# A graph and expert layer on one core: first norms, turns and weights by halves of the features, and six key tiles on the first two token tiles

## The chip, the cores and the metric

The kernel runs on one core of a Trainium2 chip. The metric is device microseconds of one execution; shown are three runs. A core has TensorE (PE; its weight loads are listed apart as PEld), VectorE (DVE), ScalarE (ACT), GpSimd (POOL) and SyncE (SP), which here only issues transfers. Each engine takes its instructions in the order in which the built program holds them, and waits on semaphores of the others.

## What is computed

A layer on 625 tokens of 1024 features, with 20000 edges: a layer norm, then two graph convolutions and a linear attention beside them, added to the input, then a second layer norm and a mixture of 8 experts with a shared one. Cut to what matters here:

```python
xn = _layernorm(x)
x = x + gnn(xn, src, dst) + mix(xn)          # two mean-over-neighbours layers; linear attention
x = x + moe(_layernorm(x))
# in mix:   k = softmax(xn @ Wk over the tokens), q = softmax(xn @ Wq over a head's features)
# in gnn:   h = relu(xn @ W_self0 + mean(xn) @ W_neigh0 + b0), then the same with W_self1, W_neigh1
# in moe:   the best 2 of 8 experts of softmax(xf @ router_w), silu(xf @ w1[e]) @ w2[e],
#           plus sigmoid(xf @ shared_gate_w) * (silu(xf @ gate) * (xf @ up)) @ shared_down
```

## The kernel before, in words

Nearly all products are made in float32r with both factors split into a high part and a rest: `split` (L98 to L99) casts the high part on ACT and subtracts it on DVE, which leaves the rest. A product is then three matmuls: high by high, high by rest, rest by high. Names ending in h and hi are high parts, in l and lo rests. `Stream` (L102 to L130) loads weights in tiles of 128x1024 through SP, three ahead, into the three buffers `wraw`, and `next()` splits the next tile into `whi` and `wlo`, three buffers of each.

Tokens come in five tiles of 128 (the last of 113). The head of the kernel, L433 to L462, is written out by hand. For each token tile `first_stats` and `first_scale` make the norm's factors on DVE (with a root on ACT), `first_norm` (L336) applies them on DVE or ACT in place in `xts`, and `first_turn` (L344, through `to_t`, L283) transposes the tile on PE in two groups of four 128x128 blocks and splits each group into `xnh` and `xnl` (features on the partitions). Before that PE runs 34 matmuls on zeros (L251) as a warm-up.

The keys' product, 8 tiles of 128 output features by Wk and 8 more by W_self0, is cut into 64 half steps (`keys_step`, L391): step s takes output tile o, token part i and half h of the features, 12 matmuls. For the first four output tiles the parts are tokens 0 to 255 and 256 to 625 (256 and 370 columns), and all four go over the first part (steps 0 to 7) before any goes over the second (8 to 15), so the first part needs two token tiles alone. Later tiles use 384 and 242 columns. The fourth tile's weights have a place of their own, `fourth`. `keys_steps` (L418) also starts, some steps behind, the exp of a finished key tile (`keys_exp`) and its transpose back (`keys_back`). `kbuf` holds four key tiles. Beside the steps DVE makes 160 pairs of one-hot tiles from the edges (`one_hots`, L493: four after each of steps 8 to 15, then three a step), which PE counts in groups of 16 (`count_group`).

The order of issue on each engine is chosen when the program is built, by a planner that takes instructions by their place in the program (higher inside `tc.high_priority()`) as soon as its own estimates say that their inputs are there. Two means bind it: `tc.keep_in_program_order` (called `keep`) puts an instruction behind the one written just before it on its engine, and `tc.issue_after(ins)` puts a block's instructions on the engine of `ins` behind `ins`. In the head all of DVE's work and all of ACT's but the copies into `kbuf` are kept; the keys' matmuls and the transposes of the edges (`turn_edges`, L354) are not.

After the second norm, `logits` (L946) makes the router's 2x16 small matmuls (20 output rows, 314 and 312 columns), after all of the first shared tile's products (L965 to L974). Experts are taken by rank in the order 0, 1, 2, 6, 3, 4, 5, 7. `expert_wide` (L1193) first makes `he` (matmuls into `pse`), splits it, then makes the second product in eight quarter steps (into `psy`, L1231 on). The next expert's rows are turned meanwhile by a `Turn` (L1016), one `step()` before each weight tile: a 32x32 transpose on DVE (L1046) into `raw`, whose split goes to ACT and POOL. An expert of 128 rows is turned on PE.

Of the kernel before, what the change touches and what calls it, by code (L numbers as in the profile page):

```python
# [19 lines left out]
N = 625  # L20
# [25 lines left out]
RANKS = (0, 1, 2, 6, 3, 4, 5, 7)  # L46
WARM = 34
# [26 lines left out]
def gps_layer(ctx: ExitStack, tc: tile.TileContext, x, src, dst,  # L74
# [27 lines left out]
    class Stream:  # L102
# [24 lines left out]
        def next(self, eng=None, into=None, **order):  # L127
            i = self.used
            self.used += 1
            self.load(max(i + self.ahead, i + 1))  # L130
            ap = self.todo[i]
            r = self.raw.pop(i)
            if into is not None:
                hi, lo = into
            else:
                hi = wts.tile([128, D], F32R, name="whi", tag="whi")
                lo = wts.tile([128, D], F32R, name="wlo", tag="wlo")
            split(r, hi, lo, eng, **order)
            b = ap.shape[2]
            return (hi.rearrange("p (a b) -> p a b", b=b), lo.rearrange("p (a b) -> p a b", b=b))  # L140
# [142 lines left out]
    def to_t(nat, t, hi, lo, order=None, both={}):  # L283
        for g in range(2):
            ps = bank("pst").rearrange("p (a b) -> p a b", b=128)
            for k in range(4):
                kt = 4 * g + k
                tr = nc.tensor.transpose(ps[:, k, rows(t)], nat[:, kt], ident[rows(t), rows(t)])
# [47 lines left out]
    def first_norm(t, eng):  # L336
        p = rows(t)
        y, z = lnt[p, 0, t:t + 1], lnt[p, 1, t:t + 1]
        if eng is nc.vector:
            keep(nc.vector.tensor_scalar(xts[p, t, :], xts[p, t, :], y, z, op0=ALU.mult, op1=ALU.add))  # L340
        else:
            keep(nc.scalar.activation(xts[p, t, :], xts[p, t, :], AF.Identity, bias=z, scale=y))

    def first_turn(t):  # L344
        return to_t(xts[rows(t), t, :].rearrange("p (k c) -> p k c", c=128), t, xnh, xnl, keep, dict(order=keep))
# [18 lines left out]
    kbuf = big.tile([128, 4, NP], F32, name="kbuf", tag="big")  # L364

    fourth = big.tile([128, 2, D], F32R, name="fourth", tag="big")
# [6 lines left out]
    def keys_back(o):  # L373
        ke = kbuf[:, o % 4, :N]
# [7 lines left out]
    def keys_exp(o):  # L382
        ke = kbuf[:, o % 4, :N]
# [7 lines left out]
    def keys_step(s):  # L391
        o, i, h = s // 4, s // 2 % 2, s % 2
        if s < 16:
            o, i = s // 2 % 4, s // 8
        if (o, i, h) == (1, 1, 0):
            wks[4] = st.next()
        if i == 0 and h == 0 and 3 < o < 2 * KT - 1:
# [4 lines left out]
        c0, n = ((0, 2 * T), (2 * T, NP - 2 * T))[i] if o < 4 else SPARTS[i]  # L402
        c, ps = slice(c0, c0 + n), kps[0]
        for kt in range(4 * h, 4 * h + 4):
            nc.tensor.matmul(ps[:, :n], wh[:, kt, :], xnh[:, kt, c], start=kt == 0, stop=False)  # L405
            nc.tensor.matmul(ps[:, :n], wh[:, kt, :], xnl[:, kt, c], start=False, stop=False)  # L406
            nc.tensor.matmul(ps[:, :n], wl[:, kt, :], xnh[:, kt, c], start=False, stop=kt == KT - 1)  # L407
        if h == 1:
            n = min(n, N - c0)
            if o < KT:  # L410
                nc.scalar.copy(kbuf[:, o % 4, c0:c0 + n], ps[:, :n])
# [17 lines left out]
    def keys_weights(o):  # L429
        wks[o] = st.next(into=(fourth[:, 0, :], fourth[:, 1, :]) if o == 3 else None, order=keep)  # L430


    with tc.high_priority():  # L433
# [27 lines left out]
        last = first_turn(4)  # L461
        keys_steps(1)  # L462
# [66 lines left out]
    while ks[0] < 8 * KT:  # L529
# [5 lines left out]
        one_hots(3)  # L535
# [6 lines left out]
    ath = atp.tile([128, NT, XP], F32R, name="ath")  # L542
# [403 lines left out]
    def logits():  # L946
        for c0, n in PARTS:
# [22 lines left out]
    to_t(by_k(xfn[rows(4), 4, :]), 4, xfh, xfl)  # L970
    ga.append(bank("psga"))
# [3 lines left out]
    logits()  # L975
# [40 lines left out]
    class Turn:  # L1016


        def __init__(self, row, n):
            self.n, self.xb, self.xs, self.left = n, expert_load(row, n), None, None  # L1020
            self.todo = [(t0, g) for t0 in range(0, n // 32, 4) for g in range(2)]

        def step(self):
# [17 lines left out]
            else:  # L1041
# [4 lines left out]
                tc.keep_in_program_order(nc.vector.transpose(  # L1046
                    raw.rearrange("p k (t r) -> p t k r", r=32), rows[:, :, k]))
# [145 lines left out]
    def expert_wide(row, n, xs, early, nxt, aside=None):  # L1193
# [5 lines left out]
        for q in range(KT // 2):  # L1199
# [24 lines left out]
            if beside:  # L1224
                nc.scalar.copy(h2[:, :, :n], s)
                for a0, b0, m in ((0, main, 128), (128, more, rest)):
                    nc.vector.tensor_sub(h2[:, :, b0:b0 + m], s[:, :, a0:a0 + m], h2[:, :, a0:a0 + m].bitcast(F32))
# [192 lines left out]
```

## Time and profile before

| | us |
|---|---|
| median of three runs | 1005.16 (1004.86 to 1005.45) |
| the profiled execution's own time | 1006.07 |
| its span, first to last instruction | 1004.5 |
| PE, PEld, DVE, ACT, POOL busy | 994.2, 860.1, 601.4, 394.4, 144.5 |

The page gives each engine's busy time as a share of the span, the granted clock (0.999 of full) and the groups of instructions by cost. A timeline line reads: start, duration, engine, line, operation, output<-inputs, shape out<-in, count of merged instructions, and in brackets the engine's idle time before and what ended it. A matmul's listed duration is longer than the distance to the next one, because they are pipelined; distances are taken from start to start.

### The profile page before, as it was taken

Reading aid. Unit: us, or ns where it says so; the run is one execution under the profiler, and the core shown is the slowest. Engines: PE = TensorE matmul, PEld = TensorE weight load, DVE = VectorE, ACT = ScalarE, POOL = GpSimd, SP = SyncE. Lnnn points to the kernel's source line nnn. Section 1 sums busy time; section 2 is a strip of 40 time slices with the busy share of each in tenths; the row PEclk is TensorE's granted clock in tenths of the full one; section 3 lists DMA queues with packets and bytes.
Section 4 is the critical chain, followed back from the end, with each engine's and each line's share of the span. In section 5 each row is a group of like instructions: output and inputs, shape, how many; then the busy total and the mean of one; then the engine's idle time right before and its main releaser. Section 6 shows DMA issues by size and latency. Waiting matters only on the chain. (4 is left out here: it accounts for less than half of the span.)

```text
span 1004.5 us, 14780 instructions
## 1 busy us (share of the span) xinstructions
PE 994.2 (99%) x5547; PEld 860.1 (86%) x5547; DVE 601.4 (60%) x1215; ACT 394.4 (39%) x577; POOL 144.5 (14%) x206
## 2 busy tenths in 40 slices
PE   9999999999999999999999999999999999999998
PEld 6999998888887779888878999997978787887886
DVE  7998745682333346423338355367678788877682
ACT  5533242231123212222116242265557576766610
POOL 1000011120100432200001002223032203110040
PEclk9999999999999999999999999999999999999999
DMA  8222227762321343322220125766977997887961
GB/s 238 60 65 64 85 100 257 251 235 86 95 84 64 105 157 124 124 83 84 66 82 2 46 81 173 241 205 207 266 244 217 292 357 237 280 297 253 339 249 64
DMA packets 111596, 164.69 MB, mean 164 GB/s; under 512 B 5948, under 2 KB 63686, under 8 KB 111512
## 3 DMA queue, kind: packets, MB, share of 16 engines
q1 hardware_dynamic: 97864, 118.38, 36.7%
q0 software_dynamic: 13456, 45.08, 13.6%
q8 instruction: 46, 0.75, 0.3%
q14 instruction: 38, 0.31, 0.1%
q10 hardware_dynamic: 192, 0.16, 0.0%
HBM read 133.19 MB, written 30.42 MB: 163 GB/s over the span
## 5 line engine op out<-in xcount | busy, mean ns | idle before, releaser
L99 DVE TENSOR_TENSOR wlo<-wraw,whi 128x1024 fp32r<-128x1024 f32 x148 | 186.0, 1257 | 247.0 <-ACT whi L99 237.8
L99 ACT CAST whi<-wraw 128x1024 fp32r<-128x1024 f32 x148 | 155.5, 1051 | 288.1 <-PE psg L211 76.2
L1215 PE MATMUL pse<-xs,whi 128*128 128x448 f32 (+1 forms) x384 | 109.2, 357 | 0.0
L99 DVE TENSOR_TENSOR wlo<-wmore,whi 128x1024 fp32r<-128x1024 f32 x67 | 82.1, 1226 | 25.8 <-ACT whi L99 23.3
L1211 PE MATMUL pse<-xs,wlo 128*128 128x224 f32 (+1 forms) x384 | 89.5, 254 | 0.6 <-DVE wlo L99 0.6
L99 ACT CAST whi<-wmore 128x1024 fp32r<-128x1024 f32 x67 | 70.4, 1051 | 42.5 <-PE psz L211 18.3
L405 PE MATMUL psk<-xnh,whi 128*128 128x384 f32 (+3 forms) x240 | 74.5, 312 | 0.3 <-ACT xnh L99 0.3
L406 PE MATMUL psk<-xnl,whi 128*128 128x384 f32 (+3 forms) x240 | 73.5, 306 | 0.6 <-DVE xnl L99 0.6
L407 PE MATMUL psk<-xnh,wlo 128*128 128x384 f32 (+3 forms) x240 | 73.5, 306 | 0.0
L1211 PEld LDWEIGHTS pse<-xs,wlo 128*128 128x128 f32 x384 | 72.0, 190 | 1.6 <-DVE wlo L99 0.8
L1215 PEld LDWEIGHTS pse<-xs,whi 128*128 128x128 f32 x384 | 69.1, 189 | 2.4
L1269 PE MATMUL psy<-whi,he 128*128 128x512 f32 (+1 forms) x176 | 69.5, 395 | 0.7 <-PEq L1304 0.7
L1270 PE MATMUL psy<-wlo,he 128*128 128x512 f32 (+1 forms) x176 | 69.4, 394 | 0.7 <-DVE wlo L99 0.7
L1271 PE MATMUL psy<-whi,he 128*128 128x512 f32 (+1 forms) x176 | 69.0, 392 | 0.0
L488 DVE TENSOR_SCALAR hot<-iota,srow,unit 125x128 f16<-125x128 f16 x160 | 49.6, 310 | 0.0
L406 PEld LDWEIGHTS psk<-xnl,whi 128*128 128x128 f32 x240 | 45.5, 190 | 0.8 <-DVE xnl L99 0.8
L405 PEld LDWEIGHTS psk<-xnh,whi 128*128 128x128 f32 x240 | 45.4, 190 | 0.6 <-ACT xnh L99 0.6
L407 PEld LDWEIGHTS psk<-xnh,wlo 128*128 128x128 f32 x240 | 45.4, 189 | 0.0
L99 POOL TENSOR_TENSOR xs<-raw,xs 128x512 fp32r<-128x512 f32 (+2 forms) x24 | 28.3, 1182 | 110.0 <-ACT xs L99 109.6
L487 DVE TENSOR_SCALAR hot<-iota,edt 125x128 f16<-125x128 f16 x160 | 39.8, 250 | 4.1 <-PE pa L505 4.1
L1269 PEld LDWEIGHTS psy<-whi,he 128*128 128x128 f32 (+1 forms) x176 | 31.9, 181 | 10.8 <-issue 1.1
L1270 PEld LDWEIGHTS psy<-wlo,he 128*128 128x128 f32 (+1 forms) x176 | 31.8, 181 | 10.0 <-DVE wlo L99 1.7
(361 smaller groups left out, 2367.2 us busy)
## 6 DMA issues: line engine op xcount, KB each, us to landing
wraw<-in_L_ffn_w_dram SPq DMA_DIRECT2D x65, 512.0 KB, 5.1
wmore<-in_L_ffn_w_dram SPq DMA_DIRECT2D x63, 512.0 KB, 5.2
xsd<-zt POOLq DMA_DIRECT2D x9, 1024.0 KB
wraw<-in_L_gnn_W_self_dram SPq DMA_DIRECT2D x16, 512.0 KB, 3.6
wraw<-in_L_gnn_W_neigh_dram SPq DMA_DIRECT2D x16, 512.0 KB, 3.8
wraw<-_ffn_shared_gate_up_dram SPq DMA_DIRECT2D x16, 512.0 KB, 3.9
wraw<-in_L_mix_Wk_dram SPq DMA_DIRECT2D x8, 512.0 KB, 6.7
wraw<-in_L_mix_Wq_dram SPq DMA_DIRECT2D x8, 512.0 KB, 3.6
```

The lines of the kernel that those rows point to most:

```text
L99: return (order(nc.scalar.copy(hi, srcap)), order((eng or nc.vector).tensor_sub(lo, srcap, hi.bitcast(F32))))
L405: nc.tensor.matmul(ps[:, :n], wh[:, kt, :], xnh[:, kt, c], start=kt == 0, stop=False)
L406: nc.tensor.matmul(ps[:, :n], wh[:, kt, :], xnl[:, kt, c], start=False, stop=False)
L407: nc.tensor.matmul(ps[:, :n], wl[:, kt, :], xnh[:, kt, c], start=False, stop=kt == KT - 1)
L487: nc.vector.tensor_scalar(h[:ET, :WIN], iota[:ET, :WIN], edst[e], None, op0=ALU.is_equal)
L488: return nc.vector.tensor_scalar(h[:ET, WIN:], iota[:ET, :WIN], srow[e], unit[e].bitcast(F32), op0=ALU.is_equal, op1=ALU.mult)
L1211: nc.tensor.matmul(ps[a][:, :n], wl[:, k, c], xs[:, kt, 0, :], start=False, stop=False)
L1215: nc.tensor.matmul(ps[a][:, :2 * n], wh[:, k, c], xs[:, kt], start=kt == 0, stop=kt == KT - 1)
L1269: nc.tensor.matmul(acc, h(kt, 0), wh[:, k, :], start=kt == 0, stop=False)
L1270: nc.tensor.matmul(acc, h(kt, 0), wl[:, k, :], start=False, stop=False)
L1271: nc.tensor.matmul(acc, h(kt, 1), wh[:, k, :], start=False, stop=kt == KT - 1)
```

## The change

- `AHEAD = 6`: six instead of four output tiles of the keys go over the first two token tiles (steps 0 to 11) before the second part (steps 12 to 23). Tiles 3 to 5 have places of their own: two in `beside`, one in `sixth`, which lies where `ath` comes later. `kbuf` holds six tiles; exp and transpose back start eight steps later.
- The order of the three kinds of matmuls inside a step changes for these tiles: by kind, four features tiles at a time.
- In the head token tiles 0 and 1 are normed by halves of the features (three halves on DVE, one on ACT), turned by halves (both tiles' first half, then both tiles' second), and the first weight tile is split by halves, the second half between the two turns. The edges' cast, the other weights, statistics and norms are moved.
- One-hots: three after each of steps 12 to 23, then three and four in turns.
- The first 16 router matmuls come before the first shared tile's last products.
- A `Turn`'s transposes on DVE are queued behind the rest of the last weight tile taken and behind the rest of the last `he`.

```diff
+AHEAD = 6
...
-        def next(self, eng=None, into=None, **order):
+        def next(self, eng=None, into=None, apart=False, **order):
...
-            split(r, hi, lo, eng, **order)
             b = ap.shape[2]
-            return (hi.rearrange("p (a b) -> p a b", b=b), lo.rearrange("p (a b) -> p a b", b=b))
+            both = (hi.rearrange("p (a b) -> p a b", b=b), lo.rearrange("p (a b) -> p a b", b=b))
+            if apart:
+
+                return both, [lambda c=slice(i * 512, (i + 1) * 512): split(r[:, c], hi[:, c], lo[:, c], eng, **order)
+                              for i in range(2)]
+            self.low = split(r, hi, lo, eng, **order)[1].ins
+            return both
...
-    kbuf = big.tile([128, 4, NP], F32, name="kbuf", tag="big")
-
-    fourth = big.tile([128, 2, D], F32R, name="fourth", tag="big")
+    kbuf = big.tile([128, AHEAD, NP], F32, name="kbuf", tag="big")
+
+    beside = big.tile([128, 4, D], F32R, name="beside", tag="big")
+    sixth = atp.tile([128, 2, D], F32R, name="sixth", tag="ath")
+    places = [beside[:, i, :] for i in range(4)] + [sixth[:, i, :] for i in range(2)]
...
-        if s < 16:
-            o, i = s // 2 % 4, s // 8
+        if s < 4 * AHEAD:
+            o, i = s // 2 % AHEAD, s // (2 * AHEAD)
         if (o, i, h) == (1, 1, 0):
-            wks[4] = st.next()
-        if i == 0 and h == 0 and 3 < o < 2 * KT - 1:
+            wks[AHEAD] = st.next()
+        if i == 0 and h == 0 and AHEAD <= o < 2 * KT - 1:
             wks[o + 1] = st.next()
...
-        c0, n = ((0, 2 * T), (2 * T, NP - 2 * T))[i] if o < 4 else SPARTS[i]
+        c0, n = ((0, 2 * T), (2 * T, NP - 2 * T))[i] if o < AHEAD else SPARTS[i]
         c, ps = slice(c0, c0 + n), kps[0]
-        for kt in range(4 * h, 4 * h + 4):
-            nc.tensor.matmul(ps[:, :n], wh[:, kt, :], xnh[:, kt, c], start=kt == 0, stop=False)
-            nc.tensor.matmul(ps[:, :n], wh[:, kt, :], xnl[:, kt, c], start=False, stop=False)
-            nc.tensor.matmul(ps[:, :n], wl[:, kt, :], xnh[:, kt, c], start=False, stop=kt == KT - 1)
+        kts = range(4 * h, 4 * h + 4)
+        terms = ((wh, xnh), (wh, xnl), (wl, xnh))
+        if s < 2:
+
+            order = [(kt, *terms[j]) for j in (0, 2, 1) for kt in kts]
+        elif i == 0 and o < AHEAD:
+            order = [(kt, *terms[j]) for j in (0, 1, 2) for kt in kts]
+        elif i == 1 and o == 0:
+            order = [(kt, *terms[j]) for j in (0, 2) for kt in kts]
+            if h == 1:
+                order += [(kt, *terms[1]) for kt in range(KT)]
+        else:
+            order = [(kt, *term) for kt in kts for term in terms]
...
-            if 10 <= k < 4 * KT + 10 and k % 4 == 2:
-                keys_exp((k - 10) // 4)
-            if 14 <= k < 4 * KT + 14 and k % 4 == 2:
-                keys_back((k - 14) // 4)
+            if 18 <= k < 4 * KT + 18 and k % 4 == 2:
+                keys_exp((k - 18) // 4)
+            if 22 <= k < 4 * KT + 22 and k % 4 == 2:
+                keys_back((k - 22) // 4)
...
         first_scale(0, 2)
-        first_norm(0, nc.vector)
-        keys_weights(0)
-        first_norm(1, nc.scalar)
-        first_turn(0)
-        first_turn(1)
+
+        lower, upper = (slice(g * 512, (g + 1) * 512) for g in range(2))
+        wks[0], halves = st.next(order=keep, apart=True)
+        for t, c in ((0, lower), (1, lower), (1, upper)):
+            first_norm(t, nc.vector, c)
+        halves[0]()
+        first_norm(0, nc.scalar, upper)
+        for g in range(2):
+            if g:
+                halves[1]()
+            for t in range(2):
+                first_turn(t, (g,))
+        keys_weights(1)
         first_stats(2)
-        keys_weights(1)
-        keep(nc.scalar.copy(edges, ei))
         keys_weights(2)
         first_scale(2, 3)
+        keep(nc.scalar.copy(edges, ei))
         keys_steps(2)
+        first_norm(2, nc.scalar)
         turn_edges()
-        first_norm(2, nc.scalar)
+        keys_weights(3)
+        first_stats(3)
         keys_steps(2)
-        first_stats(3)
+        keys_weights(4)
         first_stats(4)
-        keys_weights(3)
         first_scale(3, 5)
         keys_steps(2)
         first_norm(3, nc.vector)
+        keys_weights(5)
+        first_norm(4, nc.scalar)
         first_turn(2)
-        keys_steps(1)
-        first_norm(4, nc.scalar)
+        keys_steps(4)
         first_turn(3)
         last = first_turn(4)
-        keys_steps(1)
+        keys_steps(2)
...
-        for _ in range(8):
+        for _ in range(2 * AHEAD):
             keys_steps(1)
             with tc.issue_after(last[0].ins), tc.issue_after(last[1].ins):
-                one_hots(4)
+                one_hots(3)
...
-        one_hots(3)
+        one_hots(3 + ks[0] % 2)
...
     to_t(by_k(xfn[rows(4), 4, :]), 4, xfh, xfl)
+
+    logits(PARTS[:1])
     ga.append(bank("psga"))
     up.append(bank("psup"))
     ws_tile(xfh, xfl, ga[1:], SPARTS[1:], w=wg)
     ws_tile(xfh, xfl, up[1:], SPARTS[1:], w=wu)
-    logits()
+    logits(PARTS[1:])
...
             self.n, self.xb, self.xs, self.left = n, expert_load(row, n), None, None
+            self.behind = st.low
...
-                tc.keep_in_program_order(nc.vector.transpose(
-                    raw.rearrange("p k (t r) -> p t k r", r=32), rows[:, :, k]))
+
+                with tc.issue_after(st.low), tc.issue_after(self.behind):
+                    tc.keep_in_program_order(nc.vector.transpose(
+                        raw.rearrange("p k (t r) -> p t k r", r=32), rows[:, :, k]))
...
-                split(s, h2[:, :, :n], h2[:, :, n:])
+                low_he = split(s, h2[:, :, :n], h2[:, :, n:])[1]
         nxt = nxt()
+        nxt.behind = low_he.ins
```

More of the change, by code (lines that the diff above doesn't have):

```diff
@@ L281, in by_k, with to_t @@
         return nat.rearrange("p (c k) -> p k c", k=KT)
-    def to_t(nat, t, hi, lo, order=None, both={}):
-        for g in range(2):
+    def to_t(nat, t, hi, lo, order=None, both={}, parts=(0, 1)):
+        for g in parts:
             ps = bank("pst").rearrange("p (a b) -> p a b", b=128)
@@ L334, in first_scale, with first_norm @@
                                             op0=ALU.mult, op1=ALU.mult))
-    def first_norm(t, eng):
+    def first_norm(t, eng, c=slice(0, D)):
         p = rows(t)
@@ L339, in first_norm, with first_turn @@
         if eng is nc.vector:
-            keep(nc.vector.tensor_scalar(xts[p, t, :], xts[p, t, :], y, z, op0=ALU.mult, op1=ALU.add))
+            keep(nc.vector.tensor_scalar(xts[p, t, c], xts[p, t, c], y, z, op0=ALU.mult, op1=ALU.add))
         else:
-            keep(nc.scalar.activation(xts[p, t, :], xts[p, t, :], AF.Identity, bias=z, scale=y))
-    def first_turn(t):
-        return to_t(xts[rows(t), t, :].rearrange("p (k c) -> p k c", c=128), t, xnh, xnl, keep, dict(order=keep))
+            keep(nc.scalar.activation(xts[p, t, c], xts[p, t, c], AF.Identity, bias=z, scale=y))
+    def first_turn(t, parts=(0, 1)):
+        return to_t(xts[rows(t), t, :].rearrange("p (k c) -> p k c", c=128), t, xnh, xnl, keep, dict(order=keep), parts)
     edges = edgep.tile([EP, 2, 2 * ET], F32, name="edges")
@@ L373, in keys_back @@
     def keys_back(o):
-        ke = kbuf[:, o % 4, :N]
+        ke = kbuf[:, o % AHEAD, :N]
         for t0, n in ((0, NT - 1), (NT - 1, 1)):
@@ L382, in keys_exp @@
     def keys_exp(o):
-        ke = kbuf[:, o % 4, :N]
+        ke = kbuf[:, o % AHEAD, :N]
         mx = small.tile([128, 2], F32, name="mx")
@@ L401, in keys_step @@
         wh, wl = wks[o]
-        c0, n = ((0, 2 * T), (2 * T, NP - 2 * T))[i] if o < 4 else SPARTS[i]
+        c0, n = ((0, 2 * T), (2 * T, NP - 2 * T))[i] if o < AHEAD else SPARTS[i]
         c, ps = slice(c0, c0 + n), kps[0]
-        for kt in range(4 * h, 4 * h + 4):
-            nc.tensor.matmul(ps[:, :n], wh[:, kt, :], xnh[:, kt, c], start=kt == 0, stop=False)
-            nc.tensor.matmul(ps[:, :n], wh[:, kt, :], xnl[:, kt, c], start=False, stop=False)
-            nc.tensor.matmul(ps[:, :n], wl[:, kt, :], xnh[:, kt, c], start=False, stop=kt == KT - 1)
+        kts = range(4 * h, 4 * h + 4)
[10 more added lines that the diff above has]
+            order = [(kt, *term) for kt in kts for term in terms]
+        for j, (kt, w, xt) in enumerate(order):
+            nc.tensor.matmul(ps[:, :n], w[:, kt, :], xt[:, kt, c], start=h == 0 and j == 0,
+                             stop=h == 1 and j == len(order) - 1)
         if h == 1:
@@ L410, in keys_step @@
             if o < KT:
-                nc.scalar.copy(kbuf[:, o % 4, c0:c0 + n], ps[:, :n])
+                nc.scalar.copy(kbuf[:, o % AHEAD, c0:c0 + n], ps[:, :n])
             else:
@@ L429, in keys_weights @@
     def keys_weights(o):
-        wks[o] = st.next(into=(fourth[:, 0, :], fourth[:, 1, :]) if o == 3 else None, order=keep)
+        wks[o] = st.next(into=places[2 * o - 6:2 * o - 4] if o >= 3 else None, order=keep)
     with tc.high_priority():
@@ L539, in gps_layer @@
     assert placed == NG * CH
-    ath = atp.tile([128, NT, XP], F32R, name="ath")
+    ath = atp.tile([128, NT, XP], F32R, name="ath", tag="ath")
     degs = const.tile([128, 5, NT], F32, name="degs")
@@ L944, in gps_layer, with logits @@
     nc.gpsimd.memset(lgt[:, NP:], 0.0)
-    def logits():
-        for c0, n in PARTS:
+    def logits(parts):
+        for c0, n in parts:
             ps = bank("psr")
@@ L1226, in expert_wide @@
                 for a0, b0, m in ((0, main, 128), (128, more, rest)):
-                    nc.vector.tensor_sub(h2[:, :, b0:b0 + m], s[:, :, a0:a0 + m], h2[:, :, a0:a0 + m].bitcast(F32))
+                    low_he = nc.vector.tensor_sub(h2[:, :, b0:b0 + m], s[:, :, a0:a0 + m], h2[:, :, a0:a0 + m].bitcast(F32))
             else:
-                split(s, h2[:, :, :n], h2[:, :, n:])
+                low_he = split(s, h2[:, :, :n], h2[:, :, n:])[1]
         nxt = nxt()
+        nxt.behind = low_he.ins
         for half in range(2):
```

## The prediction

> **What bounds the kernel now.** I read the page first, then the waits of TensorE (PE), then the timelines of the four engines around each place where PE stood still.
>
> ```profile
> span 1004.5 us, 14780 instructions
> ...
> PE 994.2 (99%) x5547; PEld 860.1 (86%) x5547; DVE 601.4 (60%) x1215; ACT 394.4 (39%) x577; POOL 144.5 (14%) x206
> ```
>
> PE is busy 994.2 of 1004.5 us: time can only be won where its products stand apart by more than their own pace. That pace I took from start to start in the timeline: 0.120 us for 256 columns, 0.171 for 370, 0.174 for 384, 0.113 for 242, 0.228 for 512, 0.109 for a 128x128 transpose. Three kinds of place that the change touches show more. The first is the head, PE's timeline:
>
> ```profile
> 11.27 1.91 PE L288 MATMUL pst<-ident,xts 128*128 128x128 f32 x16
> 13.52 0.38 PE L405 MATMUL psk<-xnh,whi 128*128 128x256 f32 x1 [0.34 <-ACT xnh L99]
> 14.47 0.38 PE L406 MATMUL psk<-xnl,whi 128*128 128x256 f32 x1 [0.56 <-DVE xnl L99]
> ```
>
> The 16 transposes of token tiles 0 and 1 run from the end of the warm-up; then PE waits for the cast xnh of tile 1's lower half, does one product, and waits for the rest xnl. From 14.47 on it is dense. ACT and VectorE (DVE) there:
>
> ```profile
> 11.91 2.05 ACT L99 CAST xnh<-pst 128x512 fp32r<-128x512 f32 x4 [0.98 <-PE pst L288]
> ...
> 12.53 2.49 DVE L99 TENSOR_TENSOR xnl<-pst,xnh 128x512 fp32r<-128x512 f32 x4 [1.11 <-ACT xnh L99]
> ```
>
> The second is the end of the first shared tile (PE):
>
> ```profile
> 554.60 1.03 PE L288 MATMUL pst<-ident,xfn 113*128 113x113 f32 x8
> 555.82 0.38 PE L226 MATMUL psga<-xfh,whi 128*128 128x242 f32 x1 [0.19 <-ACT xfh L99]
> 556.03 0.28 PE L226 MATMUL psup<-xfh,whi 128*128 128x242 f32 x1
> 556.48 0.38 PE L227 MATMUL psga<-xfl,whi 128*128 128x242 f32 x1 [0.17 <-DVE xfl L99]
> ```
>
> The third is the second product of experts of rank 3 and 4 (PE, then DVE before it, then DVE at the same place of rank 5, whose follower's rows are turned on PE):
>
> ```profile
> 839.61 0.40 PE L1269 MATMUL psy<-whi,he 128*128 128x512 f32 x1
> 840.37 0.50 PE L1270 MATMUL psy<-wlo,he 128*128 128x512 f32 x1 [0.36 <-DVE wlo L99]
> ```
> ```profile
> 833.06 1.14 DVE L1046 STREAM_TRANSPOSE raw<-xb 128x512 f32<-128x512 f32 x1
> 834.12 0.28 DVE L1221 TENSOR_TENSOR set<-pse,set 128x160 f32<-128x160 f32 x1
> 834.32 1.20 DVE L1046 STREAM_TRANSPOSE raw<-xb 128x512 f32<-128x512 f32 x1
> ...
> 837.62 1.55 DVE L1227 TENSOR_TENSOR he<-set,he 128x256 fp32r<-128x256 f32 x2
> 839.10 1.21 DVE L99 TENSOR_TENSOR wlo<-wmore,whi 128x1024 fp32r<-128x1024 f32 x1
> ```
> ```profile
> 905.10 1.23 DVE L99 TENSOR_TENSOR wlo<-wraw,whi 128x1024 fp32r<-128x1024 f32 x1 [0.61 <-ACT whi L99]
> 906.24 0.55 DVE L1227 TENSOR_TENSOR he<-set,he 128x256 fp32r<-128x256 f32 x2
> 906.96 1.23 DVE L99 TENSOR_TENSOR wlo<-wmore,whi 128x1024 fp32r<-128x1024 f32 x1 [0.17 <-ACT whi L99]
> ```
>
> The next expert's transposes sit ahead of the rest of he and of the weight's rest, which PE awaits.
>
> **Part 1, the head.** The warm-up holds PE until 11.27, and its count stays. The halved norms (one of 1024 takes 0.81 on DVE; from the 160-wide op's 0.24 a half is about 0.47) and the lower half of the weight are done by 11.4, as the whole ones are now: nothing gained or lost there. The gain is in the order after the transposes. Casts come every 0.48 and rests every 0.60, so with both tiles' lower halves first the second cast, not the third, lets PE start: 12.98 plus 0.06, 13.04. Four products hi-hi, four with wlo, four with xnl (second rest done 13.81) fill 12 x 0.12 to 14.48. Meanwhile ACT puts the upper weight half (about 0.50; a whole cast follows the next by 0.95) before the last two casts, done 14.44; DVE puts its rest (0.60 against 1.12 whole) before the last two rests, done 15.62. Step 1 starts at 14.50 and its last four wait for 15.68, ending 16.16. Today these 24 products end at 17.31: **-1.15**.
>
> Then six weight tiles must be ready while tiles 0 and 1 are used; I followed the pinned order with the rows' durations. DVE: wlo of tile 1 to 16.75, statistics of token tile 2 (1.43) to 18.1, wlo of tile 2 to 19.3, its scale (0.90) to 20.1. ACT: norm of token tile 2 (1.24) to 21.4, two edge copies (0.43), weight cast of tile 3 to 22.8. DVE idles until then, and goes wlo 3 to 24.05, statistics to 25.4, wlo 4 to 26.6, statistics to 27.95, scale (1.34 with ACT's root, as 8.12 to 9.46) to 29.3, norm to 30.1, wlo 5 to 31.25. PE: steps 2 to 5 (12 x 0.12 each) to 21.9, edge transposes 0.54, token tile 2's turn 0.79, steps 6 to 9 to 29.05. The third tile's rest is there 0.1 early; the sixth's cast comes at 29.3 (its root stands before it on ACT), **+0.2**; the turns of tiles 3 and 4 (norms 30.1, 30.6) fill most of the wait for its rest at 31.25, **+0.2**. SP's queue: weight 3's load waits for the upper half's rest, 14.4 instead of 11.44, with the last x tile behind it; in today's trace that load took 5.5 to land and x 6.3, so about 20 and 21, needed at 21.8 and 26.5: no cost. Bounds of this chain, from nothing to 1.4.
>
> Key tiles 4 and 5 change from 384+242 to 256+370 columns: 0.120+0.171 against 0.174+0.113, 4 ns x 24 x 2 = **+0.19**. The Trainium skill (TensorE: Matmul & The Clock Gate, Back-to-back issue gap) puts a gap at N/2.4 plus 2.5 ns; by that the two splits cost the same, and the sum would be 0.19 lower; the rows are dearer and decide. It also has a rule against the halving: in VectorE: DVE Perf Modes, The TRN2 errata, operations from SBUF pay a fixed cost each, 58 cycles on VectorE and 224 on ScalarE. By it a cut in two adds an estimated 0.06 on DVE and 0.19 on ACT, where the rows above add 0.08 and 0.05; the sum would be 0.1 higher.
>
> One-hots start about 6 us later (last xnl about 35.4 against 29.5), 36 instead of 32 in the first stretch and 3.5 instead of 3 a step after. They cost nothing while DVE keeps up: its idle time from 60 to 130 us is 12.1, and weight rests lie 8 us and more ahead of use (60.6 for 71.4). Six key buffers, the later exp and transposes keep the same three steps between reading and overwriting. Head: -1.15+0.2+0.2+0.19, about **-0.55**; ends -1.0 and +0.4.
>
> **Part 2, the logits.** Transposes to next product takes 0.80 at 549.52, so 555.40 is due; it comes at 555.82. The next three come 0.10, 0.34 and 0.10 over the pace: 0.96, of which 0.09 stays as the change from transposes to products (550.32 to 550.58). The 16 small products put in between (0.145 each, 2.3 us, already paid later) need only tokens below 314 and the router weights, cast at 550.05. The casts and rests awaited are done by 556.97, the products come at 557.8: **-0.85** (0 if a wait moves behind them).
>
> **Part 3, the gate.** PE lost 0.53 and then 0.10 at 839.61, 0.50 and 0.11 at 875.07: 1.24. Without the early transposes DVE should run as in rank 5: its phase one ends at 903.6 there and 832.75 here, so he's rest is due at 835.9 instead of 839.18. Two transposes then take to 838.1, a third narrow one to 838.5, the weight's rest to 839.7; needed 839.84. Margin 0.1: I take **-1.2**, bounds 0 and -1.24. The later turned rows have half an expert's second product, 9 us, until used.
>
> **Sum**: -0.55-0.85-1.2 = -2.6. On the profiled execution's own 1006.07 (span 1004.5 and 1.6 around it) that is 1003.5; it lies 0.9 above the median 1005.16 of the runs, from which I give **1002.6**.
>
> **Rivals.** (a) The head gains nothing: any slip of the ping-pong of DVE and ACT (a copy of kbuf ahead of tile 3's cast, turns placed before step 10, which would wait for 30.1) takes 1.0 more: 1003.6. For it: DVE idle 2.7 us in my chain; against: the first 1.15 lies before it. (b) The planner, which places the edge transposes and products by its own estimates, keeps the former just behind step 1 as now (17.20): the edges' cast now stands behind the root of tile 2, 18.9, and PE, at 16.16, waits 2.8: 1005.4. (c) **Slower**: the gate becomes the wait. If he's rest stays where it is (839.18), the two transposes behind it (1.08+1.12) push the weight's rest to 842.6 against 839.84: 2.8 lost at two experts in place of 0.6, 1002.6+1.2+4.4 = 1008.2. It decides from he's rest at about 836.1 on; the rows of rank 5 speak against it. (d) Slower too: DVE's later one-hots push weight rests past their use, from a lag of 8 us; up to the 6 us of the late start: 1008.6. (e) Nothing slips and placement after the head happens to be denser: the head's -1.0 and some tenths more: 1001.8.
>
> **Chances**: forecast 0.48, (a) 0.19, (b) 0.09, (c) 0.08, (d) 0.03, (e) 0.13. A change of 0.2%, 2 us, is about what a measurement of this kernel can tell from none. Faster by more: most of the forecast (1002.0 to 1003.1), (e), a little of (a): 0.58; within: 0.31; slower: (c), (d): 0.11. The range 1001.4 to 1005.4 takes in (a), (b), (e) and leaves out the slower ones.
>
> **What would show it**: first psk product at 13.0, 25th at 16.2; no PE gap over 0.3 before 36 us; psr products behind the transposes at about 554 and no wait of psga; L1046 behind L1227 at every wide expert and no gap of L1270. Wrong if PE waits for whi, wlo or edges between 16 and 34 us, or for wlo after an L1046.

## The result, and the profile after

| | before | after |
|---|---|---|
| median of 11 runs each, on one chip | 1005.30 (1004.72 to 1005.64) | 1007.97 (1006.70 to 1008.79) |
| ratio, 95% interval | | 1.0023 [1.0016, 1.0031] |
| span of the profiled execution | 1004.5 | 1007.2 |

The change makes the kernel **slower** by 2.7 us, where 2.6 less was forecast. In the kernel after, the lines of the same operations are L294 (turns), L346 and L348 (norms), L363 (edge transposes), L426 (keys' products), L100 (splits), L473 (edges' cast), L1080 (turned rows), L1261 (he's rest), L1305 (second product with the rest). The page's first lines after:

```profile
span 1007.2 us, 14784 instructions
...
PE 996.0 (99%) x5547; PEld 862.1 (86%) x5547; DVE 610.7 (61%) x1218; ACT 394.5 (39%) x578; POOL 150.9 (15%) x206
```

PE's busy share says nothing of where 2.7 us went; DVE and POOL are busier by 9.3 and 6.4 us than before with nearly the same work, which becomes important further on. The list of PE's waits names the cause in its first line (what PE waited for; us in total, times, longest):

```profile
PE psed L363 <- ACT edges L473: 2.7, 1, 2.7
PE pswarm L258 <- DVE cold L255: 1.5, 1, 1.5
```

PE's timeline of the head:

```profile
11.77 1.91 PE L294 MATMUL pst<-ident,xts 128*128 128x128 f32 x16
13.54 0.62 PE L426 MATMUL psk<-xnh,whi 128*128 128x256 f32 x3
...
16.17 0.74 PE L426 MATMUL psk<-xnl,whi 128*128 128x256 f32 x4
19.57 0.66 PE L363 MATMUL psed<-ident,edges 80*125 80x80 f32 x4 [2.66 <-ACT edges L473]
20.07 0.23 PE L367 MATMUL psf<-ident,edges 80*128 80x80 f32 x1
20.09 0.72 PE L426 MATMUL psk<-xnh,whi 128*128 128x256 f32 x4
20.65 0.66 PE L426 MATMUL psk<-xnl,whi 128*128 128x256 f32 x4
21.13 1.04 PE L426 MATMUL psk<-xnh,wlo 128*128 128x256 f32 x4
21.96 1.05 PE L426 MATMUL psk<-xnh,whi 128*128 128x256 f32 x4
```

The products start 1.77 us after the first transpose and step 1 is dense to its end; then PE stands still until 19.57, for the transposes of the edges. ACT shows why they come so late:

```profile
18.72 0.29 ACT L271 ACTIVATE lnt<-lnv,epst 128x1 f32<-128x1 f32 x1 [1.37 <-DVE lnv L268]
18.92 0.59 ACT L473 CAST edges<-ei 80x500 f32<-80x500 int32 x1
```

The cast of the edges now stands behind the root of token tile 2, and the root waits for DVE's statistics. Start to start 2.82 us are lost. And the loss has a sequel: from 21.13 on four products take 0.83 to 0.86 in place of 0.48. The table by stretches (from:to and length, then busy us and, in brackets, instructions of PE, PEld, DVE, ACT and POOL; the last three columns are the granted clock, DMA share, GB/s):

```profile
16.70:19.50 2.80, 0.20 (x2) 0.00 (x0) 2.77 (x5) 1.43 (x4) 0.00 (x0) 1.00 0.87 247
19.50:21.10 1.60, 1.53 (x13) 1.54 (x14) 1.05 (x7) 0.39 (x2) 0.00 (x0) 1.00 0.59 172
21.10:24.50 3.40, 3.40 (x18) 3.40 (x17) 1.18 (x2) 2.19 (x4) 0.18 (x1) 0.50 0.49 145
```

The clock granted to PE falls to 0.50 for 3.4 us, 1.6 us after the wait has ended (21.13 against 19.57), and 18 products run where the full clock takes 31 (see the third experiment).

The second place, the logits, went as meant: small products right behind the transposes, and the shared expert's follow with no wait:

```profile
558.69 1.03 PE L294 MATMUL pst<-ident,xfn 113*128 113x113 f32 x8
559.49 0.37 PE L980 MATMUL psr<-xfh,rwp 128*20 128x314 f32 x1
...
561.88 0.27 PE L232 MATMUL psga<-xfh,whi 128*128 128x242 f32 x1
```

The third, PE, DVE and POOL at the first of the two experts:

```profile
842.64 0.40 PE L1304 MATMUL psy<-whi,he 128*128 128x512 f32 x1
843.21 0.50 PE L1305 MATMUL psy<-wlo,he 128*128 128x512 f32 x1 [0.17 <-DVE wlo L100]
```
```profile
838.39 0.56 DVE L1261 TENSOR_TENSOR he<-set,he 128x256 fp32r<-128x256 f32 x2
838.86 2.59 DVE L1080 STREAM_TRANSPOSE raw<-xb 128x512 f32<-128x512 f32 x3
841.35 1.81 DVE L100 TENSOR_TENSOR wlo<-wmore,whi 128x1024 fp32r<-128x1024 f32 x1
843.08 2.32 DVE L100 TENSOR_TENSOR wlo<-wraw,whi 128x1024 fp32r<-128x1024 f32 x1
```
```profile
840.77 4.94 POOL L100 TENSOR_TENSOR xs<-raw,xs 128x512 fp32r<-128x512 f32 x3 [19.74 <-ACT xs L100]
```

The order is the one forecast, he's rest first, and it comes in time. But the weight's rest behind the transposes takes 1.81, and the next 2.32, where 1.2 was reckoned, while POOL subtracts turned rows. PE still waits 0.34 and 0.11 here, 0.32 and 0.11 at the second expert: 0.88 in place of 1.24.

**A zero for comparing heads.** The warm-up does not end at the same time in each execution: of its 34 matmuls 6 to 14 stand 0.43 apart and the rest 0.21, so the first transpose comes between 10.14 and 11.77 us in the profiles of this study (11.27 before, 11.77 after; 10.32 in another kernel with the head of before). This scatter of 1.6 us is no effect of an edit, and it is nearly as large as the spread of the runs (1004.47 to 1006.54 in 22 runs of the kernel before). So stretches are taken from the first transpose, start to start: the head up to the first product of the queries takes 131.17 before and 134.75 after (+3.58), the shared expert up to the experts' first `psy` 138.70 and 137.78 (-0.92), the two places 1.24 and 0.88 (-0.36). Sum +2.3.

### The profile page after: what moved, and what is told of

It is laid out like the page before. It is cut to its first block, busy times and chain, and to the rows that moved or that the text cites. A ratio compares the mean times of both kernels' runs of the same rounds, so it can differ in the third digit from the quotient of the medians.

```text
span 1007.2 us, 14784 instructions
## 1 busy us (share of the span) xinstructions
PE 996.0 (99%) x5547; PEld 862.1 (86%) x5547; DVE 610.7 (61%) x1218; ACT 394.5 (39%) x578; POOL 150.9 (15%) x206
## 5 line engine op out<-in xcount | busy, mean ns | idle before, releaser
L100 DVE TENSOR_TENSOR wlo<-wraw,whi 128x1024 fp32r<-128x1024 f32 (+1 forms) x147 | 190.9, 1299 | 238.2 <-ACT whi L100 236.6
L100 ACT CAST whi<-wraw 128x1024 fp32r<-128x1024 f32 (+1 forms) x147 | 153.5, 1044 | 282.1 <-PE psg L217 76.2
L100 DVE TENSOR_TENSOR wlo<-wmore,whi 128x1024 fp32r<-128x1024 f32 x67 | 86.8, 1296 | 22.3 <-ACT whi L100 20.4
L100 ACT CAST whi<-wmore 128x1024 fp32r<-128x1024 f32 x67 | 70.4, 1050 | 42.5 <-PE psz L217 18.4
L1305 PE MATMUL psy<-wlo,he 128*128 128x512 f32 (+1 forms) x176 | 69.4, 394 | 0.3 <-DVE wlo L100 0.3
L426 PE MATMUL psk<-xnh,whi 128*128 128x384 f32 (+3 forms) x208 | 61.6, 316 | 0.0
L426 PE MATMUL psk<-xnh,wlo 128*128 128x384 f32 (+3 forms) x208 | 60.6, 311 | 0.0
L426 PE MATMUL psk<-xnl,whi 128*128 128x384 f32 (+3 forms) x208 | 60.1, 309 | 0.0
L100 POOL TENSOR_TENSOR xs<-raw,xs 128x512 fp32r<-128x512 f32 (+2 forms) x24 | 35.6, 1504 | 117.5 <-ACT xs L100 117.4
L1305 PEld LDWEIGHTS psy<-wlo,he 128*128 128x128 f32 (+1 forms) x176 | 31.8, 181 | 9.6 <-DVE wlo L100 1.2
L233 PE MATMUL psga<-xfl,whi 128*128 128x384 f32 (+1 forms) x128 | 39.2, 306 | 0.0
L233 PE MATMUL psup<-xfl,whi 128*128 128x384 f32 (+1 forms) x128 | 39.2, 306 | 0.0
L234 PE MATMUL psga<-xfh,wlo 128*128 128x384 f32 (+1 forms) x128 | 39.1, 306 | 0.0
```

Of the source, the lines that this page charges most:

```text
L100: return (order(nc.scalar.copy(hi, srcap)), order((eng or nc.vector).tensor_sub(lo, srcap, hi.bitcast(F32))))
L233: nc.tensor.matmul(ps[:, :n], wh[:, kt, :], xl[:, kt, c], start=False, stop=False)
L234: nc.tensor.matmul(ps[:, :n], wl[:, kt, :], xh[:, kt, c], start=False, stop=s)
L426: nc.tensor.matmul(ps[:, :n], w[:, kt, :], xt[:, kt, c], start=h == 0 and j == 0, stop=h == 1 and j == len(order) - 1)
L1305: nc.tensor.matmul(acc, h(kt, 0), wl[:, k, :], start=False, stop=False)
```

## The experiments

Each was timed against the kernel before on the same chip, whose median was 1005.1 to 1005.4; the ratio is to that. In the table "head" is the stretch just defined and "two places" PE's loss at the two experts, both from the profile.

| run | median, us | ratio [95%] | head | two places |
|---|---|---|---|---|
| before | 1005.3 | 1 | 131.17 | 1.24 |
| after | 1007.97 | 1.0023 [1.0016, 1.0031] | 134.75 | 0.88 |
| e1 edges cast early | 1004.38 | 0.9991 [0.9982, 1.0000] | 131.43 | 0.89 |
| e2 edges turned late | 1004.13 | 0.9988 [0.9979, 0.9997] | 131.10 | 1.13 |
| e3 twelve products in the wait | 1006.01 | 1.0009 [1.0000, 1.0018] | 133.23 | |
| e4 logits alone | 1004.38 | 0.9992 [0.9983, 1.0001] | 131.20 | 1.26 |
| e5 gate alone | 1005.61 | 1.0002 [0.9993, 1.0011] | 131.19 | 0.86 |
| e6 gate, POOL idle | 1004.05 | 0.9987 [0.9978, 0.9995] | 131.18 | none |
| e7 gate, rest first | 1005.19 | 0.9997 [0.9989, 1.0006] | 131.19 | 0.86 |
| e8 all mended | 1003.17 | 0.9979 [0.9970, 0.9989] | 130.62 | 0.86 |
| e9 all, step later | 1003.01 | 0.9975 [0.9965, 0.9986] | 130.48 | none |
| e10 four products in the wait | 1007.81 | 1.0025 [1.0016, 1.0035] | 133.21 | |
| e11 gate, step later | 1004.42 | 0.9991 [0.9981, 1.0000] | 131.18 | none |
| e12 four products, again | 1007.26 (one run) | | 134.73 | |

The theory at the start was that the head loses by the edges' wait (2.8) and by a clock that falls after it (1.5). Its rivals: the slow stretch belongs to the new order itself, or the late part of the new head is what loses.

### e1: the edges' cast back in its old place

```diff
         first_stats(2)
+        keep(nc.scalar.copy(edges, ei))
         keys_weights(2)
         first_scale(2, 3)
-        keep(nc.scalar.copy(edges, ei))
```

> The changed kernel with one line moved: the cast of the edges on ACT goes back ahead of the third weight's cast, so it no longer stands behind the root of token tile 2. Theory (the edges' wait and the clock): the cast ends at about 16.4 us, TensorE reaches the edge transposes at 16.7 without a wait, the granted clock stays at 1.00 from 16 to 25 us with products of 256 columns 0.12 apart, and 2.8 us of wait and 1.5 us of slow products go: 4.3 us below the changed kernel, about 1003.6, so 1.5 to 1.9 below the kernel before, unless the later weight tiles (4, 5 and 6), which nothing has tested yet, are late by what the prediction gave them, 0.4 us. Rival (the halved clock belongs to the new order and not to the wait): 0.50 is still granted somewhere between 17 and 30 us and only 2.8 goes, about 1005.1. Rival (the slow part moves to the sixth weight): waits of whi or wlo of 1 us and more between 25 and 34 us, about 1004.7.

Measured: 1004.38. The head falls from 134.75 to 131.43, by 3.3 of the 4.3 expected. PE goes through the edge transposes with no wait, and the granted clock is 1.00 in every stretch from 11.5 to 140 us:

```profile
15.13 0.56 PE L363 MATMUL psed<-ident,edges 80*125 80x80 f32 x4
15.53 0.23 PE L367 MATMUL psf<-ident,edges 80*128 80x80 f32 x1
15.56 0.72 PE L426 MATMUL psk<-xnh,whi 128*128 128x256 f32 x4
```

The missing 1.0 is a wait that the late edges had hidden, at the turns of token tiles 3 and 4:

```profile
27.53 0.64 PE L426 MATMUL psk<-xnh,beside 128*128 128x256 f32 x4
29.15 1.87 PE L294 MATMUL pst<-ident,xts 128*128 128x128 f32 x16 [0.98 <-DVE xts L346]
```

So both hold: the theory for 4.3, and, of the rivals, that a later part of the head is late too (1.14 from start to start), not for a weight but for a norm. With the edges mended, the new head gains nothing: 131.43 against 131.17.

### e2: the edge transposes one pair of steps later

```diff
-        turn_edges()
         keys_weights(3)
         first_stats(3)
         keys_steps(2)
+        turn_edges()
```

> The changed kernel with TensorE's edge transposes called one pair of steps later, behind the second pair of key steps in place of the first; the cast stays where the change put it. Theory (the edges' wait and the clock): the cast, done at 19.5 us, is long there when TensorE comes to the transposes at about 20; no wait, clock 1.00, about 1003.6 as with the early cast, within 0.4 of it. Rival (the clock falls anyway): about 1005.1. If only one of the two edits removes the loss, the wait on the cast was not the whole cause.

Measured: 1004.13, head 131.10, no wait for the edges, clock 1.00. A different edit removes the same loss, so it was this wait and not the place of the cast. The wait for the norm of token tile 3 is 0.70 here, because the fourth weight's cast comes earlier on ACT (20.30 against 20.64 in e1). At the second expert's place 0.59 is lost in place of 0.32; it is one profile, and what moved it was not looked into.

### e3: work in the wait

```diff
+        psx = bank("psfill")
+        for i in range(12):
+            keep(nc.tensor.matmul(psx, cold[:, :128], cold, start=i == 0, stop=i == 11))
         pse = bank("psed")
...
-            nc.tensor.transpose(pse[:ET, i, :], ...)
+            keep(nc.tensor.transpose(pse[:ET, i, :], ...))
```

> The changed kernel with 12 products of zeros (128 by 128 against 512 columns, bf16, into a bank of their own that nothing reads) between the last product of key step 1 and the edge transposes, so TensorE works through most of the wait for the edges' cast. The wait itself stays, 2.8 us: the next useful product starts at about 21.1 as in the changed kernel. Theory (the clock is lost to the idle time, apart from the wait): 1.00 is granted from 21 to 25 us, the 256-column products there stand 0.12 apart, and 1.5 us go: about 1006.5 in the changed kernel's place of 1008.0. Rival (those products are slow for another reason, such as their operands or a neighbour on the memory): the spacing of 0.21 stays and the time is that of the changed kernel, 1008.0.

Measured: 1006.01; the head falls by 1.52, to 133.23. The time to the edge transposes is the same as after (7.80 us from the first transpose in both), the stretch behind it runs at full clock:

```profile
21.10:24.50 3.40, 3.40 (x31) 3.40 (x30) 2.05 (x3) 2.60 (x5) 0.19 (x1) 1.00 0.29 82
```

31 products where the kernel after has 18 in the same stretch. The wait and the clock are two prices, 2.8 and 1.5, and useless products take the second one away. The Trainium skill (TensorE: Matmul & The Clock Gate, Part 1: The HAM clock gate) describes this gate: half or full clock only, set by how busy TensorE was in windows of about 3.4 us that run on regardless of the kernel. The trace agrees on the 0.50 and on the 3.4 us. The page's advice (Why this matters for your kernels) is to leave no idle gap over about 3 us; here an idle gap of 2.7 us was enough, and the next runs ask how much less is.

### e10 and e12: four products in the wait

The edit is that of e3 with 4 in place of 12, so that some 1.8 us in one piece stay idle.

> The changed kernel with 4 products of zeros instead of 12 ahead of the edge transposes: TensorE works 0.85 us of the wait for the edges' cast and then stands idle for about 2.0 us in one piece. Theory (the clock falls only when nearly 3 us in one piece are idle): clock 1.00 from 21 to 25 us, time as with 12 products, about 1006.1. Rival (2.0 us are already enough, or the share of idle time in a longer stretch counts): 0.50 is granted for 3.4 us after the wait and the time is the changed kernel's, 1007.6 to 1008.

Measured: the profiled execution took 1005.24 with a clock of 1.00, the other eight runs 1007.2 to 1008.1. Neither answer holds for all runs, and there is a trace of the shorter one alone. So the same kernel was profiled again:

> The kernel with 4 products of zeros in the wait once more, for a second profile: its profiled execution took 1005.24 with a clock of 1.00 throughout, its other eight runs 1007.2 to 1008.1, and no trace shows what those did. Theory (2.0 us without work let the clock fall in most runs, by where a counting window of the clock happens to lie): this profile shows 0.50 for about 3.4 us after the wait, products of 256 columns 0.21 apart, and takes 1007 or more. Rival (the eight runs were long for another reason): the clock is 1.00 from 15 to 30 us, and if the run takes 1007 or more, the time lies elsewhere in the trace.

Measured: 1007.26. Stretches of e10 (first line) and of e12:

```profile
18.70:21.50 2.80, 2.80 (x25) 2.80 (x25) 0.48 (x3) 2.20 (x4) 0.18 (x1) 1.00 0.74 208
```
```profile
16.80:18.60 1.80, 0.03 (x2) 0.02 (x1) 1.76 (x4) 0.79 (x2) 0.00 (x0) 1.00 0.88 247
19.20:22.60 3.40, 3.40 (x18) 3.40 (x17) 0.70 (x4) 2.56 (x4) 0.18 (x1) 0.51 0.57 161
```

The two executions have the same idle time (1.78 and 1.77 us) and differ by 1.52 us in the head, the price of the half clock. So an idle time of 1.8 us can let the clock fall and need not.

What decides stays open. By the trace's record of the clock it goes to full at 4.60 us in e10, 5.49 in e12 and 7.47 in the kernel after, during the warm-up. From there, in e12 and in the kernel after, it stays full for 13.65 us and then halves for 3.413, a quarter of that: 19.14 to 22.55 and 21.13 to 24.54. That fits a decision by windows of 3.413 us. Counted so, 1.86 us of the wait after the change lie in the window 17.71 to 21.13. But in e12 (window 15.73 to 19.14) and in e10 (14.84 to 18.25) the idle time lies whole inside one window alike, with PE busy for 1.57 and 1.56 us of it by the profile, and the clock falls in e12 alone. Neither the idle time nor its place against the windows tells the two apart. What fills the rest of the window differs: in e12 all of the edge transposes, in e10 four products of the keys and the first of the transposes. Whether that decides, no run shows.

### e4: the logits alone

```diff
-    def logits():
-        for c0, n in PARTS:
+    def logits(parts):
+        for c0, n in parts:
...
+    logits(PARTS[:1])
     ga.append(bank("psga"))
...
-    logits()
+    logits(PARTS[1:])
```

> The kernel before with the one edit of the logits: the router's products for tokens below 314 stand behind the transposes of the last tokens, ahead of the last 242 columns of the shared expert. Theory: 0.85 to 0.9 us below the kernel before, about 1004.4 (ratio 0.9991), with products of psr right behind the eight transposes at about 558 and no wait of psga there. Rival (the wait moves behind the small products): no change, 1005.3.

Measured: 1004.38, and 137.77 against 138.70 for the shared expert's stretch, -0.93. By the traces this part is right alone and in company; the interval of the medians' ratio (0.9983 to 1.0001) just takes in no change.

### e5: the gate alone

The edit is the change's own: `issue_after` around the transposes of `Turn.step`, nothing else.

> The kernel before with the third part alone: the turned rows' transposes of the next expert stand behind the rest of he. Theory (DVE and POOL slow each other): he's rest comes in time, the three transposes follow, then the weight's rest takes 1.8 us beside POOL's subtraction of the turned rows in place of 1.2, and TensorE waits 0.34 for it at the two experts where it waited 0.5 for he: 0.2 us gained at each, 0.4 in all, about 1005.0. Rival (the prediction's step): 1.2 gained, 1004.2.

Measured: 1005.61, no change that the interval can tell (0.9993 to 1.0011); the two places lose 0.86 in place of 1.24. DVE's rows are those of the kernel after: 1.80, 2.33 and 1.48 for the three rests beside POOL. So the third part is worth 0.4 at most and not 1.2, whatever the head does.

### e6: the gate, with POOL idle

```diff
-                self.left = (raw, xs[:, k, 0, c], xs[:, k, 1, c], nc.gpsimd)
+                self.left = (raw, xs[:, k, :, c])
...
+            if self.left and len(self.left) == 2:
+                raw, both = self.left
+                nc.scalar.copy(both, raw[:, :, None, :].to_broadcast(list(both.shape)))
...
```

> The third part alone, and POOL takes no part in turning the rows: ACT writes the turned rows into both places in one copy of twice the size, and the subtraction that makes the low part is left out (the low part holds the row itself, so the experts' output is not the reference's). Theory (DVE and POOL slow each other): with POOL idle the weight's rest behind the three transposes takes 1.2 us again, not 1.8, TensorE's wait for it goes from 0.34 to at most 0.1, and the gain is about the prediction's, 1.0 to 1.2: 1004.2. Rival (the subtraction is slow because of its own operands or of the transposes ahead of it): 1.8 stays and the time is that of the third part alone, about 1005.0. ACT has 0.4 us more per transposed block, which may put a later cast of a weight on the path; the row's duration decides then, not the time.

Measured: 1004.05, and no loss at the two places. DVE behind the transposes:

```profile
835.47 2.56 DVE L1052 STREAM_TRANSPOSE raw<-xb 128x512 f32<-128x512 f32 x3
837.95 1.19 DVE L99 TENSOR_TENSOR wlo<-wmore,whi 128x1024 fp32r<-128x1024 f32 x1
840.09 1.23 DVE L99 TENSOR_TENSOR wlo<-wraw,whi 128x1024 fp32r<-128x1024 f32 x1 [0.95 <-ACT whi L99]
```

The transposes take what they took (2.56 against 2.58), the rests are back at 1.2. It is POOL's subtraction that made them slow.

### e7: the gate, with the weight's rest ahead of the narrow transpose

```diff
+                wh, wl = st.next()
                 if half or u:
                     nxt.step()
-                wh, wl = st.next()
```

> The third part alone, with the next expert's step called behind the fetch of the weight in place of ahead of it, so that the weight's rest stands ahead of the third, narrow transpose on DVE (two transposes stay ahead of it). Theory: the rest starts 0.4 us earlier and is still slow beside POOL, 1.6 to 1.8, but is done just as TensorE comes to it: the waits go to 0.1 at most and about 1.0 is gained against the kernel before, 1004.3. Rival (the second weight's rest, now behind the narrow transpose, becomes late in its place): 1005.0.

Measured: 1005.19, still 0.86 at the two places: a miss. The rest starts ahead of the narrow transpose, as meant, and takes 2.11 in place of 1.80. Set POOL's three subtractions beside DVE:

```profile
837.52 2.11 DVE L99 TENSOR_TENSOR wlo<-wmore,whi 128x1024 fp32r<-128x1024 f32 x1
839.56 0.40 DVE L1048 STREAM_TRANSPOSE raw<-xb 128x128 f32<-128x128 f32 x1
839.89 1.99 DVE L99 TENSOR_TENSOR wlo<-wraw,whi 128x1024 fp32r<-128x1024 f32 x1
841.80 1.48 DVE L99 TENSOR_TENSOR wlo<-wmore,whi 128x1024 fp32r<-128x1024 f32 x1
```
```profile
837.25 1.30 POOL L99 TENSOR_TENSOR xs<-raw,xs 128x512 fp32r<-128x512 f32 x1 [19.88 <-ACT xs L99]
...
838.50 2.29 POOL L99 TENSOR_TENSOR xs<-raw,xs 128x512 fp32r<-128x512 f32 x1
...
840.76 1.44 POOL L99 TENSOR_TENSOR xs<-raw,xs 128x128 fp32r<-128x128 f32 x1
```

POOL's first ends at 838.55; DVE's rest, issued within it, ends 1.08 later, at 839.63. POOL's second, issued at 838.50, ends 1.16 after that, at 840.79; DVE's next rest ends 1.09 after this, at 841.88, and so on. They do not share: each waits out the other's whole instruction. That is why starting the rest earlier gained nothing: it ended 2.38 after POOL's first start, as in e5 (836.88 to 839.26). The transpose in between, with one input, took 0.40 beside POOL as elsewhere. The Trainium skill (SBUF — State Buffer, Who interferes with whom) states just this: a VectorE instruction with two inputs from SBUF contends with a GpSimd instruction that reads SBUF, one with a single input and outside the two-port modes does not, and the later of the two is blocked until the other has finished. These rows agree on each of the three points.

### e11: the gate, with the first step one weight later

```diff
-                if half or u:
+                if half or u > 1:
                     nxt.step()
```

(on top of e7, so that one transpose alone stands ahead of the rest and POOL's first subtraction is not ready before it)

> The kernel before with the third part in the form with the weight's rest ahead, and the next expert's first step one weight later. Theory (DVE and POOL take turns): both places lose their waits, 1.1 to 1.25 against the kernel before, 1004.2, about what the third part without POOL gave (1004.05). Rival (later rests become late): 1005.2 as without the later step.

Measured: 1004.42, and no loss at the two places, with POOL doing all of its work:

```profile
835.54 1.17 DVE L1048 STREAM_TRANSPOSE raw<-xb 128x512 f32<-128x512 f32 x1
836.64 1.18 DVE L99 TENSOR_TENSOR wlo<-wmore,whi 128x1024 fp32r<-128x1024 f32 x1
837.74 1.20 DVE L1048 STREAM_TRANSPOSE raw<-xb 128x512 f32<-128x512 f32 x1
838.87 1.19 DVE L99 TENSOR_TENSOR wlo<-wraw,whi 128x1024 fp32r<-128x1024 f32 x1
840.58 1.73 DVE L99 TENSOR_TENSOR wlo<-wmore,whi 128x1024 fp32r<-128x1024 f32 x1 [0.52 <-ACT whi L99]
```

```profile
837.45 1.52 POOL L99 TENSOR_TENSOR xs<-raw,xs 128x512 fp32r<-128x512 f32 x1 [19.66 <-ACT xs L99]
839.67 1.55 POOL L99 TENSOR_TENSOR xs<-raw,xs 128x512 fp32r<-128x512 f32 x1 [0.69 <-ACT xs L99]
```

Rests that take two inputs and transposes that take one alternate. POOL's first subtraction waits for the end of the first rest (837.82) and then runs beside a transpose, which takes 1.20 as without it. The second waits for the end of the second rest (840.06) and holds up the third (1.73), where PE has time. By these rows the 1.2 of the forecast were there to be had, with another order; the medians differ by 0.7, with an interval from 0 to 1.9.

### e8: all mended

The edits of e2 and e7 on the kernel after, and:

```diff
-        keys_weights(3)
         first_stats(3)
+        keys_weights(3)
```

> The changed kernel with three edits: the edge transposes one pair of key steps later (as tried before), the statistics of token tile 3 ahead of the fourth weight's rest on DVE, which stood idle for 2.25 us there, and the weight's rest ahead of the narrow transpose in the experts. Theory: the norm of token tile 3 is done at about 27.4 us in place of 28.7, TensorE at 28.1 no longer waits for it (0.7), and 0.7 to 0.8 goes at the two experts: about 1.4 below the changed kernel with late edge transposes, 1002.7. Rival (token tile 3 has not landed when its statistics are wanted, so the fourth weight's rest is late behind them): 1003.5 or more, with a wait of TensorE for that rest before 25 us.

Measured: 1003.17; the head is 130.62, 0.48 less than in e2 where 0.7 was expected, and PE's turns of tiles 3 and 4 start with no wait, at 28.05, the norm being done at 27.4. The experts' share was missed for the reason that e7 shows.

### e9: the same, with the step one weight later

> The kernel with all three edits, and the next expert's first step one weight later in the experts' second product, so that only one transpose stands ahead of the weight's rest that TensorE waited for, and POOL's first subtraction is ready only when that rest has begun. Theory (the two engines take turns, whole instruction by whole instruction, when both read two operands from SBUF): the rest takes 1.2 and is done 1.5 us ahead of its use, the two waits of 0.55 a place go (0.33 and 0.1 at each of two experts), 0.9 in all: 1002.3. Rival (the subtractions, now all behind it, make the following weights' rests late in their turn): waits of 0.3 and more at the next two weights, about 1003.2 as without the edit.

Measured: 1003.01 (8 runs, 1002.00 to 1003.45), ratio 0.9975 [0.9965, 0.9986]: 2.1 to 2.5 us below the kernel before, the fastest of all here. The two places lose nothing. By the traces, first transpose to last product, it takes 986.39 against 989.23 before and 991.48 after: 2.84 less than before, about what had been forecast for the change. Against e8 the medians gain 0.2 where the places give 0.9; with the scatter of the warm-up in 8 runs the medians can't tell the two. Also, one wait of the experts for a weight, at about 815 us before (0.70 there), varies between 0 and 0.7 from profile to profile with no edit near it, and blurs such sums.

## Why the prediction was wrong, point by point

**Head, order behind the transposes, -1.15: right.** First product 1.77 us after the first transpose, as worked out; step 1 ends after 4.98 (e1: 4.97), forecast 4.89, against 6.04 before: -1.07.

**Head, the chain behind it: the step that failed.** The prediction says "PE: steps 2 to 5 (12 x 0.12 each) to 21.9, edge transposes 0.54", and so took it that PE makes the edge transposes after step 5. PE has them behind step 1, where they stood before, and the cast that they need had been moved behind the root of tile 2: 2.82. This was rival (b), seen and priced at 2.8, and given 0.09. Nothing in the profile spoke for so low a chance: the rows of before have the transposes at the end of step 1, with the cast done in time, and the new text still calls them there.

```profile
14.77 0.63 ACT L444 CAST edges<-ei 80x500 f32<-80x500 int32 x1
```
```profile
17.31 0.56 PE L357 MATMUL psed<-ident,edges 80*125 80x80 f32 x4
```

The order that is in the row should have been the forecast, and a new order the rival.

**The price of that wait, 2.8: too small.** It was priced as a plain shift. After it the clock falls for 3.4 us, 1.5 more. The trace of before held the same behaviour in its warm-up, where the first 12 matmuls stand 0.43 apart, but the rival's price did not ask what an idle PE does to what follows.

**The late weights, +0.4: covered, then wrong in kind.** In the kernel after PE comes 4 us late to them and waits for none. With the edges mended (e1, e2) PE waits 1.14 and 0.70, for the norm of tile 3 and not for the sixth weight: rival (a), "turns placed before step 10", at about its price of 1.0. The new head is then 0.26 longer (e1) or 0.07 shorter (e2) than the head before. Only a third edit (e8, e9) brings it to -0.55 and -0.69, the forecast's -0.55.

**Column split, +0.19: not separated.** The head's sum closes with it: -1.07 + 2.82 + 1.52 + 0.19 = 3.46 of 3.58.

**Logits, -0.85: right.** -0.92 in company, -0.93 alone.

**Gate, -1.2: mis-sized, measured -0.36 (e5: -0.38).** he's rest and the three transposes end as worked out (he's rest at 838.95; less the 3.03 by which the trace is late there, 835.9, as forecast). The term that failed is "the weight's rest to 839.7", that is 1.2 for a subtraction beside POOL: it took 1.81. The rows of before showed the cause: he's rest, priced from undisturbed rows at 0.55, took 1.55 there (837.62 to 839.17), beside POOL, and this excess was put down to the transposes ahead of it.

```profile
836.95 2.14 POOL L99 TENSOR_TENSOR xs<-raw,xs 128x512 fp32r<-128x512 f32 x2 [0.70 <-ACT xs L99]
```

**Sum.** Forecast -2.6, measured by the traces +2.25. The difference of 4.85 is 2.82 + 1.52 for the edges, 0.84 for the gate, -0.4 for late weights that were not felt, and 0.1 for the rest. Slower had 0.11, from rivals (c) and (d); neither occurred. The measured time lies 2.6 above the range, because the edges' case was cut off at 2.8 with nothing for its sequel, and the cases were not combined.

## What to carry to other kernels

When a producer is moved, look up where its consumer stands in the order that the trace shows, and forecast that order unless something binds another. A wait of two or three microseconds on TensorE can cost more than its length, here 1.52 us more: ask what the clock does behind it, and price two cases together where both can hold. Two engines that both read two operands from SBUF, VectorE and GpSimd, took turns by whole instructions here (e7); before counting a subtraction at its usual time, look what GpSimd does in the same microseconds.

## What was not expected of the hardware

- After an idle time of 1.77 us (e12) and of 2.66 us (after) in one piece the clock granted to PE was 0.50 for 3.4 us, starting 0.6 and 1.6 us after the work had begun again, and costing 1.52 us (18 products of 256 columns in place of 31). With 1.78 us in e10 it stayed at 1.00, and what makes the difference is open. Idle times of 0.54 and 0.98 us (e2, e1) left it at 1.00.
- The first transpose, behind 34 fixed warm-up matmuls, came 10.14 to 11.77 us into the span, as 6 to 14 of them stood 0.43 us apart in place of 0.21.
- DVE's subtraction of 128x1024 takes 1.2 us alone and 1.5 to 2.3 beside POOL's subtractions of turned rows; DVE's transpose of 128x512, with one input, takes 1.20 beside one of them (e11) and 1.17 without.
